# A state-space, attention and expert block on one core: the first scan block spread by TensorE, another softplus, and the causal mask on GpSimd

## The chip, the core and the metric

The kernel runs on one core of a Trainium2 chip. A core has TensorE for matrix products (PE; its weight loads, PEld, overlap them), VectorE (DVE), ScalarE (ACT), GpSimd (POOL) and SyncE (SP). Each engine works through its own list of instructions in order, and waits on semaphores for what other engines or transfers deliver. DMA transfers are issued from the queues of SP, ACT and POOL. The on-chip memory has 128 partitions; a tile written "128x512" has 512 elements in each of them. PE writes into the banks of a second memory, PSUM, from which ACT and DVE read.

The metric is the time of one execution in microseconds of the device. A profile records one execution; its span goes from the first to the last instruction.

## The reference

Input is x of 4 sequences, 1024 tokens, 128 channels. Three parts follow each other:

```python
# 1: state space (256 inner channels, 16 states), then layernorm(x + ...)
xz = x @ in_proj_w.T;  xb, z = split(xz)
xb = silu(conv_b + sum_k xpad[:, k:k+L] * conv_w[:, k])        # 4 taps
dt_in, B, C = split(xb @ x_proj_w.T)                           # 1, 16, 16
dt = softplus(dt_in * dt_w[:, 0] + dt_b)
dA = exp(dt[..., None] * -exp(A_log))
h[t] = dA[t] * h[t-1] + (xb * dt)[t] * B[t]                    # scan over tokens
y = layernorm(sum_n h * C + xb * D_param) * silu(z)
x = layernorm(x + y @ out_w.T)
# 2: attention, 16 heads of 8 channels, causal
s = (layernorm(x) -> q, k, v);  scores = q @ k.T;  scores[above the diagonal] = -max
hidden = x + softmax(scores) @ v @ o_w + o_b
# 3: 16 experts, two per token, at most 512 tokens each, 512 hidden
x = layernorm(x + hidden + experts(layernorm(hidden)))
```

## The kernel before

**Order.** No part of the order is left to the compiler. Each operation is registered with a planner (`Plan`, methods of `Emit` such as `pe`, `act`, `tt`, `scan`, `dma`), with a due time `v` as its first argument, an estimated duration and the tiles that it reads and writes. `Plan.schedule` is a list scheduler: whenever an engine comes free in its model, the ready operation with the lowest `v` is taken; for ACT an operation that needs another table of functions counts as later. The outcome is one list for each engine, issued in that order. Tiles come from pools with few slots, so an operation also waits for a slot. After the fact `Plan.run` puts filler matmuls (zeros, L1560) into gaps of PE of 800 ns or more, once the constants for them are there and while an accumulating group is open.

There are two plans. `before_branch` loads weights, makes the first of eight "fronts", and works out a bound on the attention scores (matmuls against `one_col`, a root as a power on POOL, a maximum, `mild`). Then the program branches on `mild`. `mild_path` holds the second plan: all the rest.

**A front** (`front`, 512 tokens): the convolution as four products with `w_tap` for each of two blocks of 128 channels, Silu on ACT; two products for the gate z with Silu; `xproj`, copied from PSUM as `proj` (row 0 is dt_in, rows 1 to 32 are B and C); for each channel block the `dt` product with `w_dt`, then softplus: DVE adds the bias and takes the minimum with 40 (`dtmin`, L450), ACT does Exp and Ln(1 + .), DVE takes the maximum of that and the biased input (`dt`, L457), then u = xb * dt (L437). xb, silu(z), dt, u, B and C go to DRAM (L368, by SP).

**Scans** (`scans`, nine units: seven of 512 tokens and two of 256). A partition holds one of 32 channels and one of 4 states. For each half m of the channels `dt` and `u` are read back from DRAM, each row repeated over 4 partitions (`dt_sp`, `u_sp`); B and C come likewise, repeated over the channels (`bt`, `ct`). For each group g of 4 states: one product u * B of 128x2048 on DVE, four Exp(dt * a) on ACT (`da`), four scans on DVE (L463), a copy of the state, one product h * C of 128x2048 on DVE, and products on PE with `sel` that sum over the states. The layernorms use a power of -0.5 on POOL (`rr`), which DVE's L457 and ACT then use.

**Attention.** A block of 128 keys against up to 512 queries: for groups of four heads, scores on PE into PSUM (L390), Exp on ACT into `pr` (L417), then products with v into an accumulating bank (`av`). On diagonal blocks a second product, the identity times `mask_k` (-1e38 above the diagonal, made by POOL at L1623), is added to the scores for each head:

```python
calls.append(("mm", pst[:, jj, :w], kk[:, j0 + jj, :], q[:, j0 + jj, q0:], True, not diag))
if diag:
    calls.append(("mm", pst[:, jj, :P], fx(identb), fx(mask_k), False, True))
```

Attention of a unit runs behind its scans, beside the scans of later units; what is left after the last scan runs by itself. From unit 6 (`DVE_FROM`) some copies may be taken by DVE or ACT, as the planner finds them free. `post`, `route` and `sends` follow for each unit: POOL sends token rows to the experts' buffers by indirect DMA (L2010). After all units come the experts, the fetch of their results (L2111) and the last layernorm.

Of the kernel before, what the change touches and what calls it, by code (L numbers as in the profile page):

```python
# [9 lines left out]
F32 = mybir.dt.float32  # L10
# [8 lines left out]
P = 128  # L19
# [36 lines left out]
TABLE = 1283  # L56
# [81 lines left out]
class Op:  # L138
    __slots__ = ("v", "engs", "emit", "deps", "succ", "left", "ready", "start", "end", "done", "eng", "allocs",
                 "uses", "table", "name", "wire", "seq", "opens", "closes")  # L140


class Plan:
# [17 lines left out]
    def add(self, v, engs, emit, outs, ins, name="", table=None, wire=0, free=(), after=()):  # L161
# [3 lines left out]
        op.opens = op.closes = None  # L165
        op.start = op.end = op.done = op.eng = None
# [27 lines left out]
    def schedule(self):  # L194
# [65 lines left out]
        times, queued = [0.0], {0.0}  # L260

# [7 lines left out]
        while n_left:  # L269
# [8 lines left out]
            while again:  # L278
                again = False
                for e in engines:  # L280
# [3 lines left out]
                    for op in waiting[e]:  # L284
# [6 lines left out]
                        if e == "ACT" and op.table and op.table != table:  # L291
                            v += 100.0
                        if best is not None and (v, op.seq) >= best[:2]:
                            continue
# [23 lines left out]
                    op.end = t + dur  # L318
                    op.done = op.end
# [17 lines left out]
    def run(self):  # L337
        order = self.schedule()
        last, ready, groups = 0.0, False, {}
        with self.tc.manual_schedule():  # L340
            for op in order:
                if op.eng == "PE":
                    gap = op.start - last
                    if ready and groups and gap >= FILL_GAP:
                        view = next(iter(groups.values()))
                        for _ in range(int(gap / FILL_STEP)):
                            self.fill(view)
                    last = op.end
                op.emit(op.eng)
                ready = ready or op is self.fill_after  # L350
                if op.opens is not None:
                    groups[id(op.opens.buf)] = op.opens
                if op.closes is not None:
                    groups.pop(id(op.closes.buf), None)


class Emit:
# [12 lines left out]
    def pe(self, v, calls, share=1, name="", group=None, last=False):  # L370
        nc = self.nc
        dur, outs, ins = 0.0, [], []
        for kind, out, lhsT, rhs, start, stop in calls:
# [7 lines left out]
            dur += one / 0.92 / share  # L381
            outs.append(out)
# [9 lines left out]
        op = self.p.add(v, {"PE": dur}, emit, outs, ins, name)  # L392
        if group is not None:
            op.opens, op.closes = (None, group) if last else (group, None)
# [34 lines left out]
    def _dve(self, v, emit, outs, ins, cols, per=1.0, fixed=None, name="", pool=False):  # L429
        if fixed is None:  # L430
            fixed = 125 if any(x.psum for x in outs + ins) else 62
        return self.p.add(v, {"POOL" if pool else "DVE": (fixed + per * cols / 0.96) * (2.2 if pool else 1)}, emit, outs, ins, name)

    def tt(self, v, out, a, b, op, pool=False, name=""):
        eng = self.nc.gpsimd if pool else self.nc.vector
        fixed = 600 if op == ALU.pow else None
# [41 lines left out]
    def memset(self, v, out, value, pool=False, name=""):  # L478
        eng = self.nc.gpsimd if pool else self.nc.vector
        return self._dve(v, lambda e: eng.memset(out.real(), value), [out], [], out.cols, name=name, pool=pool)  # L480
# [15 lines left out]
def mamba_then_moe_block_kernel(ctx: ExitStack, tc: tile.TileContext, a: dict, out: bass.AP):  # L496
# [847 lines left out]

    plan_a = Plan(nc, tc)
# [36 lines left out]
    conv_b, dt_b = small("f_conv_b", [P, NC2]), small("f_dt_b", [P, NC2])  # L1382
# [8 lines left out]
    def fronts_of(p, e, n_dt):  # L1391
# [9 lines left out]
        W = dict(w_in=fx(w_in), w_tap=fx(w_tap), w_xp=fx(w_xp), w_dt=fx(w_dt), conv_b=fx(conv_b), dt_b=fx(dt_b))  # L1401

        def front(f, v, step):
# [9 lines left out]
            xb = []  # L1413
            for c in range(NC2):
                pt = p.new(pool["bank"])
                e.pe(v + step, [
# [4 lines left out]
                e.act(v + 2 * step, t, pt, AF.Silu, bias=W["conv_b"][:, c : c + 1], name="xb")  # L1421
                e.dma(v + 7 * step, fx(chan["xb"][f])[c * P : (c + 1) * P, :], t, name="xb_d")
                xb.append(t)
            for c in range(NC2):
                pt = p.new(pool["bank"])
                e.pe(v + 2 * step, [("mm", pt, W["w_in"][:, DI + c * P : DI + (c + 1) * P], xT[:, NTAP - 1 :], True, True)], name="zmm")
                t = p.new(pool["sz"])
                e.act(v + 2 * step, t, pt, AF.Silu, name="sz")
                e.dma(v + 6 * step, fx(chan["sz"][f])[c * P : (c + 1) * P, :], t, name="sz_d")
            pt = p.new(pool["bank"])  # L1430
            e.pe(v + 3 * step, [("mm", pt, W["w_xp"][:, c, :], xb[c], c == 0, c == NC2 - 1) for c in range(NC2)], name="xproj")
            proj = p.new(pool["proj"])
            e.act(v + 3 * step, proj, pt, AF.Copy, name="proj")
            e.dma(v + 4 * step, fx(bc_h[f]).rearrange("s g i t -> (s g i) t"), proj[1 : 1 + 2 * NS, :], name="bc_d")
            for c in range(NC2):
# [3 lines left out]
                b1 = W["dt_b"][:, c : c + 1]  # L1439
                e.ts(v + 4 * step, ex, pt, b1, DT_MAX, ALU.add, ALU.min, name="dtmin")  # L1440
                e.act(v + 5 * step, ex, ex, AF.Exp, name="sp_exp")
                e.act(v + 5 * step, ex, ex, AF.Ln, bias=fx(one_col), name="sp_ln")
                dt = p.new(pool["dt"])
                e.stt(v + 6 * step, dt, pt, b1, ex, ALU.add, ALU.max, name="dt")
                e.dma(v + 6 * step, fx(chan["dt"][f])[c * P : (c + 1) * P, :], dt, name="dt_d")
                u = p.new(pool["u"])
                e.tt(v + 6 * step, u, xb[c], dt, ALU.mult, name="u")
                e.dma(v + 6 * step, fx(chan["u"][f])[c * P : (c + 1) * P, :], u, name="u_d")
        return front

    def before_branch():
        p, e = plan_a, ea
        fx = p.fixed
        for t, value in ((mean_col, 1.0 / DI), (one_col, 1.0), (neg_half, -0.5)):
            e.memset(0, fx(t), value, name="memset")
        def load(v, t, src, queue="SP"):
# [11 lines left out]
        load(2.2, w_dt, fx(a["dt_w"]))  # L1468
        load(2.3, dt_b, fx(a["dt_b"]).rearrange("(n p) -> p n", p=P))
        for k in range(NTAP):  # L1470
            e.tt(2, fx(w_tap)[:, k, :], fx(w_in)[:, 0:DI], fx(conv_w)[:, :, k], ALU.mult, name="w_tap")
        front = fronts_of(p, e, 2)
        front(0, 0.5, 2.5)

        pn = ps.single[0][:, 0:8].rearrange("p (t s g) -> p t s g", t=2, s=2)
        for s, w in enumerate((wq_pad, wk_pad)):
            sqw = fx(bnd[s])
            e.ts(3, sqw, fx(w), fx(ln1_w), None, ALU.mult, name="sqw")
            e.tt(3, sqw, sqw, sqw, ALU.mult, name="sqw")
            for g in range(GQ):  # L1480
                e.pe(9, [("mm", fx(pn)[:, 0, s, g : g + 1], sqw[:, g, :], fx(one_col), True, True),
# [754 lines left out]
```

## Time and profile before

| | us |
|---|---|
| median of nine runs | 1120.28 (1117.57 to 1127.39) |
| the profiled execution | 1122.07 |
| its span, first to last instruction | 1120.2 |
| mean granted clock of PE | 0.899 of full speed |
| busy: PE, DVE, ACT, POOL | 907.2, 792.9, 708.1, 226.4 |

The page's second part shows the same in 40 slices of 28 us, a digit for each tenth that an engine is busy:

```profile
PE   6378789478999999999999879999868882999920
DVE  2567989998999999999999969997404113111146
ACT  3377687256997995887997659897445561443411
POOL 2010001201001001470001430101331103455532
```

Slices 1 and 2 are the start, up to slice 28 the scans run (DVE), then the rest of attention, and from slice 35 the experts (PE). The tables of functions on ACT are loaded 35 times, 1.283 us each. In the views that follow, an arrow "out<-in" names the tiles by the program, "x4" counts instructions that were merged into a line, and a bracket gives how long the engine had been idle and what ended that.

### The profile page before, as it was taken

How to read it: one execution, taken by the hardware profiler on the slowest of the kernel's cores; microseconds unless marked ns; L12 is line 12 of the kernel's file. 1: busy time of each engine (PE TensorE's matmuls, PEld its weight loads, DVE VectorE, ACT ScalarE, POOL GpSimd, SP SyncE). 2: the span in 40 equal slices, each digit the busy share in tenths (PEclk: the TensorE clock that was granted, in tenths of full speed). 3: DMA queues.
4: the chain of work that ended last, by engine and by line, in shares of the span. 5: the costliest groups of instructions: out<-in, count | busy, mean ns of one | idle time of the engine just before them, and what ended most of it. 6: DMA issues, size and time to landing. Idle time of an engine off the chain costs nothing.

```text
span 1120.2 us, 17031 instructions
## 1 busy us (share of the span) xinstructions
PE 907.2 (81%) x6136; PEld 452.4 (40%) x6136; DVE 792.9 (71%) x1390; ACT 708.1 (63%) x1069; POOL 226.4 (20%) x337
## 2 busy tenths in 40 slices
PE   6378789478999999999999879999868882999920
PEld 2123234124434336434335423445535441777710
DVE  2567989998999999999999969997404113111146
ACT  3377687256997995887997659897445561443411
POOL 2010001201001001470001430101331103455532
PEclk9588989688999998999999989999889785999965
DMA  3775686485663654482653544339623212322153
GB/s 101 263 181 201 200 294 220 169 267 156 204 183 98 191 176 118 148 248 86 202 182 106 170 110 131 107 114 290 210 81 87 69 32 67 114 71 80 48 154 94
DMA packets 152757, 168.65 MB, mean 151 GB/s; under 512 B 23635, under 2 KB 105814, under 8 KB 152534
## 3 DMA queue, kind: packets, MB, share of 16 engines
q1 hardware_dynamic: 146262, 158.63, 47.0%
q0 software_dynamic: 4096, 8.43, 2.2%
q8 instruction: 50, 0.82, 0.3%
q10 hardware_dynamic: 2304, 0.40, 0.2%
q14 instruction: 45, 0.37, 0.1%
HBM read 110.20 MB, written 57.21 MB: 149 GB/s over the span
## 4 chain that ended last, share of the span: by engine, by line
PE 45%; DVE 25%; ACT 11%; DMA 7%; issue 6%; another core or an unknown queue 2%; POOL 1%; SPq 1%; DVEq 0%; ACTq 0%; POOLq 0%
PE bank L390 23%; PE pair L390 20%; DVE arena L463 10%; DVE arena L437 10%; ACT arena L417 9%; DVE arena L457 2%; PE bank L388 2%; SPq L368 1%; DMA arena<-in_fc_w_dram 1%; DVE smalls L487 1%; DMA xin<-rt_full 1%; DMA arena<-u_h 1%; DMA q_parts<-halves 1%; DMA eout<-rt_full 1%
## 5 line engine op out<-in xcount | busy, mean ns | idle before, releaser
L417 ACT ACTIVATE arena<-pair 128x1024 f32<-128x1024 f32 (+2 forms) x336 | 299.2, 923 | 93.3 <-PE pair L390 65.2
L437 DVE TENSOR_TENSOR arena<-arena 128x2048 f32<-128x2048 f32 (+2 forms) x155 | 305.6, 1989 | 11.8 <-DMA arena<-u_h 11.7
L417 ACT ACTIVATE arena<-arena,f_a_neg 128x512 f32<-128x512 f32 (+1 forms) x288 | 187.7, 675 | 80.0 <-DVE arena L463 63.2
L390 PE MATMUL pair<-arena 128*128 128x256 bf16 (+3 forms) x864 | 196.4, 317 | 30.2 <-ACT arena L417 23.3
L437 POOL TENSOR_TENSOR smalls<-smalls,neg_half 128x4 f32<-128x4 f32 (+2 forms) x35 | 52.7, 1505 | 633.4 <-DVE smalls L448 566.1
L390 PE MATMUL bank<-arena,vp 128*32 128x256 f32 (+3 forms) x1728 | 168.0, 470 | 9.6 <-ACT arena L417 6.9
L463 DVE TENSOR_TENSOR_SCAN arena<-arena,state 128x512 f32<-128x512 f32 (+1 forms) x160 | 160.6, 1051 | 0.0
L463 DVE TENSOR_TENSOR_SCAN arena<-arena 128x512 f32<-128x512 f32 x128 | 150.1, 1209 | 0.1
L390 PEld LDWEIGHTS <-arena 128*128 128x128 bf16 x864 | 80.4, 99 | 164.5 <-issue 141.8
L390 PE MATMUL pair<-mask_k,identb 128*128 128x128 bf16 x512 | 95.9, 221 | 0.0
L390 PE MATMUL bank<-arena,f_sel 128*32 128x512 f32 x512 | 72.2, 639 | 28.5 <-DVE arena L437 28.5
L2010 POOL DMA_INDIRECT xin<-xrow,rt_put x64 | 77.9, 1216 | 80.9 <-issue 35.3
L417 ACT ACTIVATE arena<-pair,b 128x512 f32<-128x512 f32 x64 | 40.5, 683 | 71.4 <-PE pair L390 68.7
L390 PE MATMUL pair<-xT,f_w_tap 128*128 128x512 f32 x128 | 64.6, 654 | 21.8 <-DMA xT<-in_xT_dram 17.9
L2111 POOL DMA_INDIRECT eout<-arena,to x64 | 61.3, 957 | 67.7 <-DVE arena L437 49.5
L390 PEld LDWEIGHTS bank<-arena,vp 128*32 128x32 f32 x1728 | 38.4, 110 | 70.0 <-issue 46.4
L388 PE MATMUL bank<-ident,arena 128*128 128x128 f32 x256 | 44.0, 299 | 27.9 <-DMA arena<-xin 15.9
L390 PEld LDWEIGHTS bank<-arena 128*128 128x128 f32 x512 | 59.8, 192 | 5.6 <-issue 4.3
L390 PE MATMUL bank<-arena 128*128 128x128 f32 x512 | 61.2, 277 | 0.5 <-ACT arena L417 0.4
L417 ACT ACTIVATE arena<-arena,smalls 128x128 f32<-128x128 f32 x73 | 30.3, 483 | 48.3 <-DVE smalls L457 44.0
L437 DVE TENSOR_TENSOR arena<-bank,arena 128x512 f32<-128x512 f32 (+1 forms) x25 | 16.7, 666 | 61.7 <-PE bank L390 61.7
L390 PE MATMUL pair<-arena,arena 128*128 128x512 f32 x128 | 59.2, 606 | 0.0
(184 smaller groups left out, 1090.7 us busy)
## 6 DMA issues: line engine op xcount, KB each, us to landing
arena<-k_parts SPq DMA_DIRECT2D x52, 288.0 KB
arena<-bc_h SPq DMA_DIRECT2D x56, 256.0 KB
arena<-dt_h SPq DMA_DIRECT2D x56, 256.0 KB
arena<-u_h SPq DMA_DIRECT2D x56, 256.0 KB
arena<-in_fc_w_dram SPq DMA_DIRECT2D x32, 256.0 KB
q_parts<-halves SPq DMA_DIRECT2D x21, 384.0 KB
k_parts<-halves SPq DMA_DIRECT2D x21, 384.0 KB
arena<-q_parts SPq DMA_DIRECT2D x28, 288.0 KB
```

The source lines that it names most:

```text
L368: return self.p.add(v, {queue: 460}, lambda e: engine.dma_start(out.real(), in_.real()), [out], [in_], name, wire=wire, after=after)
L388: nc.tensor.transpose(out.real(), lhsT.real(), rhs.real())
L390: nc.tensor.matmul(out.real(), lhsT=lhsT.real(), rhs=rhs.real(), start=start, stop=stop)
L417: nc.scalar.activation(out.real(), in_.real(), func, scale=real(scale), **kw)
L437: return self._dve(v, lambda e: eng.tensor_tensor(out.real(), a.real(), b.real(), op), [out], [a, b], out.cols, fixed=fixed, name=name, po ...
L457: return self._dve(v, lambda e: nc.vector.scalar_tensor_tensor(out.real(), a.real(), real(s), b.real(), op0, op1), [out], self._views(a, s ...
L463: return self._dve(v, lambda e: nc.vector.tensor_tensor_scan(out.real(), d0.real(), d1.real(), real(init), ALU.mult, ALU.add), [out], self ...
L487: self._dve(v, lambda e: nc.vector.bn_stats(s.real(), x.real()), [s], [x], 128, name=name + "_bn")
L2010: inst = nc.gpsimd.indirect_dma_start(out=dst.real()[:, :], out_offset=bass.IndirectOffsetOnAxis(ap=idx.real(), axis=0), in_=src.real(), i ...
L2111: inst = nc.gpsimd.indirect_dma_start(out=eo_d.real()[:, :], out_offset=bass.IndirectOffsetOnAxis(ap=idx.real(), axis=0), in_=src.real(), ...
```

## The change

Six things are changed together.

- *Softplus.* The bias dt_b becomes row 33 of `w_dt`, and `proj` gets a row of ones by an Identity with a column of the identity as bias. Then softplus is max(x, 0) + ln(1 + exp(-|x|)): ACT does Abs, Exp with scale -1 and Ln; `dtmin` on DVE is gone.
- *Front 0* is cut in two: `conv_half` stays ahead of the branch, `dt_half` moves behind it (`adopt` takes over its two tiles). The chain of `mild` gets earlier due times, the loads of `A_log` go from ACT's queue to SP's, and the Exp of `a_all` waits for both Silu of the convolution.
- *The first block of scans* (unit 0, m = 0) gets dt and u not from DRAM but by PE: `wide` is the identity with each column repeated four times, so a product spreads 32 rows over 128 partitions. For the first g the Exp and the products with B read that from PSUM; copies go to the tiles that later g read. Front 1 waits for it. In the built order dt and u are loaded in 68 transfers each instead of 72.
- *Mask.* The 512 mask products and their weight loads are gone. After the Exp, POOL sets `pr` above the diagonal to 0 in place (`keep_below`); from unit 6 the planner may give that to DVE. In the built order POOL does 164 (152 of them before the last scan: 102 of 256 columns, 50 of 512) and DVE 20, 19 of them after the last scan.
- *The planner* models PE's clock (`Clock`), chooses fillers while it schedules (544 filler products instead of 456, 56 of them ahead of the first work of front 0), lets ACT hold its table for 3 us before it changes, and has other estimates for powers and memsets on POOL. Table loads go from 35 to 19.
- Some small operations on POOL (`tokcol`, `pad`) get other due times.

```diff
-TABLE = 1283
+TABLE, HOLD = 1283, 3000
...
                         if e == "ACT" and op.table and op.table != table:
                             v += 100.0
+                            if t < op.ready[e] + HOLD:
+                                wake(op.ready[e] + HOLD)
+                                continue
...
+                    if e == "PE":
+                        gap = t - last
+                        if ready and (groups or spare) and gap >= FILL_GAP:
+                            op.fillers = int(gap / FILL_STEP)
+                            clock.fill(last, gap, op.fillers)
...
+    def keep_below(self, v, x, lower, dve=False, name=""):
+        nc, n = self.nc, x.shape[1]
+        engs = {"POOL": 130 + 1.05 * x.cols}
+        if dve:
+            engs["DVE"] = 62 + x.cols / 0.96
+
+        def emit(e):
+            if e == "POOL":
+                nc.gpsimd.affine_select(out=x.real(), in_=x.real(), compare_op=ALU.is_ge, fill=0.0, base=0,
+                                        pattern=[[0, n], [1, P]], channel_multiplier=-1)
+            else:
+                nc.vector.tensor_tensor(x.real(), x.real(), lower.real().unsqueeze(1).to_broadcast([P, n, P]), ALU.mult)
+
+        return self.p.add(v, engs, emit, [x], [x] + ([lower] if dve else []), name)
...
-            e.act(v + 3 * step, proj, pt, AF.Copy, name="proj")
+            e.act(v + 3 * step, proj, pt, AF.Identity, bias=fx(ident)[:, 1 + 2 * NS : 2 + 2 * NS], name="proj")
...
-                b1 = W["dt_b"][:, c : c + 1]
-                e.ts(v + 4 * step, ex, pt, b1, DT_MAX, ALU.add, ALU.min, name="dtmin")
-                e.act(v + 5 * step, ex, ex, AF.Exp, name="sp_exp")
+                e.act(v + 4 * step, ex, pt, AF.Abs, name="sp_abs")
+                e.act(v + 5 * step, ex, ex, AF.Exp, scale=-1.0, name="sp_exp")
                 e.act(v + 5 * step, ex, ex, AF.Ln, bias=fx(one_col), name="sp_ln")
                 dt = p.new(pool["dt"])
-                e.stt(v + 6 * step, dt, pt, b1, ex, ALU.add, ALU.max, name="dt")
+                e.stt(v + 6 * step, dt, pt, 0.0, ex, ALU.max, ALU.add, name="dt")
...
+        load(2.2, w_dt[n_row : n_row + 1], fx(a["dt_b"]).unsqueeze(0))
...
-        front = fronts_of(p, e, 2)
-        front(0, 0.5, 2.5)
+        conv_half, _, _ = fronts_of(p, e, 2)
+        conv_half(0, 0.5, 2.5)
...
-            e.dma(20, a_all[:, j, :], fx(a["A_log"])[j * NR : (j + 1) * NR, :].unsqueeze(1).to_broadcast([NR, NI, NS]),
-                  queue="ACT", name="a_all")
+            e.dma(4, a_all[:, j, :], fx(a["A_log"])[j * NR : (j + 1) * NR, :].unsqueeze(1).to_broadcast([NR, NI, NS]),
+                  name="a_all")
...
-        e.act(21, a_all, a_all, AF.Exp, name="a_all")
+        e.act(21, a_all, a_all, AF.Exp, name="a_all").deps.add(conv_half.last[1][1])
...
+        xb_first = [adopt("xb") for _ in range(NC2)]
+        first = dt_half(0, 0.0, 2.0, xb_first, kept=(0,))
...
+                    spread = own and g == 0
+                    if spread:
+                        wide = new("tmp", "wide")
+                        e.copy(1, wide.rearrange("p (m i) -> p m i", i=NI), fx(ident).unsqueeze(2).to_broadcast([P, P, NI]), name="wide")
+                    for j in range(J if spread else 0):
+                        lhsT = wide[:, j * P : (j + 1) * P]
+                        for src, dst, k in ((first[0][0], dts[j], 0), (first[0][1], us[:, j, :], 1)):
+                            pb = new("bc")
+                            mm = e.pe(12 + 0.1 * j + 0.05 * k, [("mm", pb, lhsT, src, True, True)], name="spread")
+                            if k:
+                                e.tt(12 + 0.1 * j, h[:, j, :], pb, bt[g], ALU.mult, name="uB")
+                            else:
+                                d_first.append(new("da"))
+                                ex = e.act(12 + 0.1 * j, d_first[j], pb, AF.Exp, scale=fx(a_neg)[:, j, 0:1], name="da")
+                            e.act(14 + j, dst, pb, AF.Copy, dve=True, name="spread_c")
+                    for conv, gate in second_front if spread else ():
+                        conv.deps.add(mm)
+                        gate.deps.add(ex)
...
-                            calls.append(("mm", pst[:, jj, :w], kk[:, j0 + jj, :], q[:, j0 + jj, q0:], True, not diag))
-                            if diag:
-                                calls.append(("mm", pst[:, jj, :P], fx(identb), fx(mask_k), False, True))
+                            calls.append(("mm", pst[:, jj, :w], kk[:, j0 + jj, :], q[:, j0 + jj, q0:], True, True))
...
+                        if diag:
+                            half = pr[:, 0:per, :P]
+                            e.keep_below(vv + 0.1 * j0 + dv * 0.4, half, fx(lower), dve=u >= DVE_FROM, name="mask")
```

## The prediction

> **What bounds the kernel now.** I first cut the span into stages by the first and last instruction of each kind: scans run from 47.25 to 773.8 us, the last front ends near 192, the experts start near 949. The busy time of each engine in each stage (window; length, then PE, weight load, DVE, ACT, POOL with instruction counts; clock, DMA share, GB/s):
>
> ```profile
> 44.85:195.00 150.15, 125.95 (x408) 51.61 (x412) 127.66 (x126) 107.15 (x143) 11.13 (x9) 0.90 0.71 226
> 195.00:742.50 547.50, 483.78 (x3610) 216.59 (x3598) 525.70 (x709) 422.96 (x657) 90.82 (x90) 0.94 0.53 161
> 742.50:948.80 206.30, 157.50 (x1385) 87.70 (x1383) 79.39 (x324) 109.39 (x163) 42.51 (x77) 0.84 0.39 113
> 948.80:1071.00 122.20, 121.37 (x696) 88.25 (x696) 17.99 (x37) 47.20 (x73) 62.56 (x120) 0.99 0.27 79
> ```
>
> DVE is busy 525.7 of 547.5 us in the second row, so DVE sets the pace there although PE has more busy time over the whole kernel. In the first row DVE idles 22.5 us, in the third PE works through attention left over, in the fourth PE is full. The page's chain of waits says the same (PE 45%, DVE 25%, ACT 11%). Second view, what DVE waits for between 45 and 756 us (total, times, longest):
>
> ```profile
> DVE arena L450 <- PE pair L390: 15.7, 4, 6.3
> DVE arena L437 <- DMA arena<-u_h: 11.7, 1, 11.7
> DVE arena L457 <- ACT arena L417: 7.5, 10, 2.1
> DVE arena L450 <- ACT arena L417: 2.7, 1, 2.7
> ```
>
> L450 is the `dtmin` of a front: DVE works its list in order, so scans behind it stand while it waits for the front's matmul. The `u_h` wait is the start, and the timeline shows it:
>
> ```profile
> 31.41 1.28 DVE L437 TENSOR_TENSOR arena<-arena 128x512 f32<-128x512 f32 x2
> 34.70 2.48 SPq L368 DMA_DIRECT2D arena<-dt_h  x4
> 37.28 2.49 SPq L368 DMA_DIRECT2D arena<-u_h  x4
> 44.85 2.29 DVE L437 TENSOR_TENSOR arena<-arena 128x2048 f32<-128x2048 f32 x1 [11.73 <-DMA arena<-u_h]
> 47.25 4.57 DVE L463 TENSOR_TENSOR_SCAN arena<-arena 128x512 f32<-128x512 f32 x4
> ```
>
> The first `u` is made by 32.7 us, but its way through DRAM lets the first long DVE instruction start at 44.85 only.
>
> **The terms**, against the profiled execution's span of 1120.2 us.
>
> *1. Start: -15.* In the new order, from rows of before: first conv at 10.87 (the 16 instructions of both channel blocks took 7.12, so 3.56 a block), its Silu 0.69, second conv 3.56 behind that Silu's bank, Silu 0.69: 19.4. Table load 1.28 and the `a_all` Exp 0.31: 21.0. Branch, 0.8 us from `mild` written (24.26) to the branch's first instruction (25.04): 21.8. `proj` 0.58, `dt` matmul 1.9 (3.78 for both blocks): 24.3. Abs 0.60, Exp 0.63, second Abs 0.60, Ln 0.66: 26.8. L457 0.74 and `u` 0.66: 28.2. Spread matmul 0.9 (two instructions of 7.12/16), multiply from PSUM 0.68: the first scan stands at 30 instead of 47.25. Then each of the four channel groups needs an Exp from PSUM (0.68) and copies (6 of 8 on ACT, 0.6 to 0.7), about 2.5 us a group against 1.12 a scan, so the fourth scan ends near 38.8 instead of 51.82, with the second step's multiply (2.27) already used as filling: -13 to -18, taken -15. It falls to -10 if the first B rows, which still come by DRAM, are late (loads of this kind took 3.0 to 7.5 us from issue to use, and seven loads stand before them on SP), or if the 56 new filler matmuls ahead of the first conv leave the clock lower: 16 passes took 9.47 us cold at 45.91, 7.12 at 10.87.
>
> *2. Front stalls: -14.* The 14 `dtmin` in the branch go, and with them 15.7 + 2.7 = 18.4 us of waits. ACT's Abs reads the matmul instead. What is late next is L457, which needs the Ln; it waited 7.5 us in ten pieces. ACT in the first row gains 14 x 0.60 = 8.4 for Abs and loses 16 table loads of 1.283 = 20.5 (38.4 before), so it is no nearer its bound. I keep a quarter of the waits, at L457; the ends are -4 (they mostly move there) and -20.
>
> *3. DVE's own work: -8.6.* 14 x 0.743 (the row of L450 `dtmin`) = -10.4; the first product as 4 x 0.68 instead of 2.29: +0.4; two spread copies on DVE, 2 x 0.69: +1.4. DVE is the pace-setter, so this counts in full while it stays so.
>
> *4. Mask on PE: -4.* 512 mask matmuls go, each with a weight load. What one takes on PE is the spacing, not its 221 ns of mean duration:
>
> ```profile
> 768.91 0.22 PE L390 MATMUL pair<-arena 128*128 128x128 bf16 x1
> 768.97 0.22 PE L390 MATMUL pair<-mask_k,identb 128*128 128x128 bf16 x1
> 769.03 0.22 PE L390 MATMUL pair<-arena 128*128 128x128 bf16 x1
> ```
>
> 0.06 from start to start. The 384 in the scan stage (21 us of PE) free nothing: DVE covers them. Without that cover they would be worth the 21. The 128 behind it are on the path of the third row: 128 x 0.055 = -7. Against that stand new masks between Exp and the value matmul, 12 on POOL and 19 on DVE; where 12 groups end on such a block I let 0.25 us each show, after the 0.28 row below: +3. Ends -7 and +6, if half of 31 masks show 0.4 us in full.
>
> *5. POOL beside DVE: +20.* The open cost. 152 masks lie on POOL in the scan stage: 102 of 256 columns, 50 of 512. No row of before has such an instruction there. The nearest of its kind and the nearest of its situation:
>
> ```profile
> 26.30 0.28 POOL L1623 TENSOR_SCALAR_AFFINE_SELECT mask_k<-mask_k 128x128 bf16<-128x128 bf16 x1
> 59.53 1.25 DVE L463 TENSOR_TENSOR_SCAN arena<-arena 128x512 f32<-128x512 f32 x1
> 59.64 1.21 POOL L476 COPY arena<-arena 1x64 f32<-1x64 f32 x1
> 60.70 1.24 DVE L463 TENSOR_TENSOR_SCAN arena<-arena 128x512 f32<-128x512 f32 x1
> 60.80 1.21 POOL L476 COPY arena<-arena 1x64 f32<-1x64 f32 x1
> 61.86 1.24 DVE L463 TENSOR_TENSOR_SCAN arena<-arena 128x512 f32<-128x512 f32 x1
> ```
>
> Scans alone start 1.12 us apart (four in 4.55 at 105.97); beside these 64-column copies 1.165: each copy costs DVE 0.045, and itself stretches until the scan ends. Lower bound, that much per mask whatever its width: 152 x 0.045 = 7. By width, 0.18 for 256 and 0.36 for 512 columns: 102 x 0.18 + 50 x 0.36 = 36. Upper bound, the whole moving part at the rate of the 128-column row over POOL's cheapest row of 0.14: (0.28 - 0.14)/128 = 1.1 ns a column, so 102 x 0.28 + 50 x 0.56 = 57. A mask can only take time between two DVE instructions that would have followed without a gap: in the new order 195 of DVE's 357 long instructions in this stage are followed directly by another long one. I take 36 x 195/357 = 20, nearest to the row by width.
>
> The Trainium skill speaks against this change in "SBUF — State Buffer", section "Who interferes with whom": a DVE instruction with two SBUF inputs and a GpSimd instruction that reads SBUF exclude each other, for the whole instruction. The trace agrees that POOL stretches (a 128x8 power took 2.47 us beside scans), but the scans beside that power kept their pace, 2.33 us for two, so no whole power of over 1 us was held against DVE. By the rule in full (0.14 more for each of 152 masks than the upper bound) the term would be 57 + 21 = 78 and the sum +39; by the row it is the 20 above.
>
> *6. POOL's queue: +3.* The masks stand in POOL's list between 35 powers of the normalisations and 64 sends. DVE's L457 waits for a power; that wait was 1.1 us before. If every power stood behind one mask of 0.5 us it would be 35 x 0.5 = 18; the powers have due times ahead of DVE's use, so 3, ends 0 and 18. The sends feed the experts after 949 and have slack until then.
>
> *At nothing:* the eight `A_log` loads moved to SP (ahead of the front's stores, seven took 4.55 us of ACT's queue; SP waits for the front's data at that time anyway, and without that cover they are 5 us at the start, inside term 1's bound); 88 more filler matmuls (in PE gaps; PE is not the bound before 742); table loads in the scan stage, covered by DVE.
>
> Sum: -15 - 14 - 8.6 - 4 + 20 + 3 = -18.6, span 1101.6. The execution took 1.87 us beyond its span and lies 1.8 above the median, so as a median 1101.7, given as 1102. The gains are 41.6 us: the masks eat them when one costs 41.6/152 = 0.27 us of DVE.
>
> **Rivals.**
> A, slower: POOL holds DVE for the whole moving part of every mask (57 instead of 20): -18.6 - 20 + 57 = +18.4, 1139. For it: copies stretch to the scan's end, so the two do exclude each other. Against: the scans beside powers. It decides from 0.27 us a mask.
> B: the cost is per mask and not per column (7): 1120.2 - 31.6, as a median 1089. For it: the power rows, which hold DVE for next to nothing whatever their length.
> C: the stalls only move. ACT's chain Abs, Exp, Ln, shared with the scans' own Exps, leaves L457 waiting (-4), and the start is bound by the B rows (-10): -10 - 4 - 8.6 - 4 + 23 = -3.6, 1117, at the edge of no change. For it: L457 already waited ten times for ACT.
>
> **How the numbers follow.** Forecast 0.40 (its own range 1094 to 1110), A 0.20, B 0.28, C 0.12. About 0.3%, 3.4 us, is what a measurement tells from no change (the nine runs spread 0.9%). Faster: 0.40 + 0.28 + 0.04 of C = 0.72; same: 0.06 of C and 0.02 of A = 0.08; slower 0.20. All low ends together give 1075, all high ones far above A; the range 1078 to 1137 holds B and most of A and leaves out about 2 in 10.
>
> **What would show it.** First scan at about 30 us and the fourth's end near 39; no wait of DVE for the matmul in the front stage, and less than 10 us at L457; DVE's busy time in scans and 128x2048 products up by some 20 us in total or gaps that end with masks (A: nearly 60; B: under 10); masks on POOL of 0.4 and 0.7 us alone and over 1 us beside DVE; waits for powers below 5 us; the stretch from the last scan to the experts about 4 us shorter than 175. The forecast is wrong if scans spread to over 1.4 us beside masks, or if the first scan comes after 36.

## The result, and the profile after

| | before | changed |
|---|---|---|
| median, us | 1119.58 (31 runs) | 1144.48 (10 runs) |
| ratio, 95% interval | | 1.0212 (1.0181 to 1.0243) |
| span of the profiled execution | 1120.2 | 1139.1 |
| first scan starts, last scan ends | 47.25, 773.8 | 35.41, 807.9 |
| last scan to first product of the experts | 172.9 | 158.6 |

Slower by 25 us by the medians. In the two traces the start is 11.8 us earlier and the end of the scans 34 us later; 14 us of that come back behind them. The stages again, cut in the same way (length, then PE, weight load, DVE, ACT, POOL with counts; clock, DMA share, GB/s):

```profile
44.85:195.00 150.15, 124.55 (x466) 50.54 (x465) 131.02 (x135) 103.87 (x158) 13.78 (x9) 0.93 0.71 229
195.00:760.00 565.00, 470.13 (x3090) 187.29 (x3089) 515.06 (x668) 401.99 (x616) 255.17 (x221) 0.94 0.48 146
760.00:967.00 207.00, 157.67 (x1346) 81.61 (x1344) 106.95 (x357) 117.44 (x182) 67.20 (x103) 0.88 0.41 121
967.00:1090.00 123.00, 121.11 (x691) 87.50 (x690) 17.31 (x36) 48.72 (x75) 61.77 (x118) 0.99 0.27 78
```

In the second row DVE now idles 49.9 us (565.0 - 515.06) where it idled 21.8, and POOL is busy 255 us where it was 91. (Of the 21.8, 9.0 are a single wait of L457 at 656 us that the profile puts to "remote". The prediction's view of waits leaves it out, and the trace of the same kernel on another chip, b_before, has no such wait.) The groups of the changed kernel by shape, DVE's long ones and then POOL's masks:

```profile
L474 DVE TENSOR_TENSOR arena<-arena 128x2048 f32<-128x2048 f32 x127 | 292.4, 2316 | 8.8 <-issue 7.5 <-PE bank L426 1.2
L500 DVE TENSOR_TENSOR_SCAN arena<-arena 128x512 f32<-128x512 f32 x128 | 156.1, 1251 | 0.3
L500 DVE TENSOR_TENSOR_SCAN arena<-arena,state 128x512 f32<-128x512 f32 x96 | 120.5, 1297 | 0.0
L500 DVE TENSOR_TENSOR_SCAN arena<-arena,state 128x256 f32<-128x256 f32 x64 | 46.4, 768 | 1.2 <-ACT arena L454 1.2
...
L527 POOL TENSOR_SCALAR_AFFINE_SELECT arena<-arena 128x256 f32<-128x256 f32 x104 | 104.9, 1024 | 248.0 <-ACT arena L454 246.8 <-DMA arena<-bc_h 0.7 <-DMA arena<-dt_h 0.2
L527 POOL TENSOR_SCALAR_AFFINE_SELECT arena<-arena 128x512 f32<-128x512 f32 x60 | 80.5, 1355 | 106.4 <-ACT arena L454 104.9 <-DVE smalls L505 1.4
```

Before, the four DVE groups had means of 2275, 1209, 1265 and 729 ns: each long instruction is 32 to 42 ns longer in the mean, and the longest scan takes 1.65 us where it took 1.28. A mask of 256 columns takes 0.40 us at the least and 1.02 in the mean, one of 512 columns 0.63 and 1.36. What DVE waits for between 45 and 774 us:

```profile
DVE smalls L509 <- PE bank L424: 19.8, 9, 5.6
DVE arena L494 <- ACT arena L454: 12.9, 10, 2.8
DVE arena L494 <- PE bank L426: 7.6, 5, 2.5
DVE arena L474 <- issue: 7.5, 1, 7.5
DVE rt_full L485 <- DMA xin<-rt_full: 3.8, 3, 2.6
DVE smalls L494 <- POOL smalls L474: 3.7, 3, 2.0
```

The waits of `dtmin` are gone. New at the top is L509, the reciprocal of a softmax's sum (0.6 us before): it needs attention's products with v, and those wait for masks. The timeline shows one such place, a short one:

```profile
281.30 0.41 POOL L527 TENSOR_SCALAR_AFFINE_SELECT arena<-arena 128x256 f32<-128x256 f32 x1 [0.23 <-ACT arena L454]
...
282.54 7.06 POOL L527 TENSOR_SCALAR_AFFINE_SELECT arena<-arena 128x256 f32<-128x256 f32 x4 [0.84 <-ACT arena L454]
...
284.04 2.29 DVE L474 TENSOR_TENSOR arena<-arena 128x2048 f32<-128x2048 f32 x1
...
286.65 0.84 PE L426 MATMUL bank<-arena,vp 128*32 128x384 f32 x4 [1.57 <-POOL arena L527]
...
288.12 1.94 ACT L454 ACTIVATE arena<-pair 128x1024 f32<-128x1024 f32 x2 [2.93 <-POOL arena L527]
...
291.63 0.26 DVE L509 RECIPROCAL smalls<-bank 128x16 f32<-128x16 f32 x1 [0.95 <-PE bank L424]
```

Four masks take 7.06 us beside DVE's products and scans. PE waits for one; ACT waits 2.93 us, because its next exponentials need a buffer that POOL still holds; 9 us after the first of these masks DVE stands at the reciprocal, with scans queued behind it.

The longest waits arise where POOL issues its sends (`DMA_INDIRECT`, 1 to 3 us each, two batches of 16 before the last scan). POOL works in order too, so a mask behind sends waits for them, and with it the product with v:

```profile
474.33 1.88 POOL L2110 DMA_INDIRECT xin<-xrow,rt_put  x1 [0.21 <-DVE arena L500]
...
476.51 1.93 POOL L2110 DMA_INDIRECT xin<-xrow,rt_put  x1 [0.22 <-issue]
...
478.46 1.69 POOL L527 TENSOR_SCALAR_AFFINE_SELECT arena<-arena 128x256 f32<-128x256 f32 x1
...
480.21 3.53 PE L426 MATMUL bank<-arena,vp 128*32 128x512 f32 x8 [10.04 <-POOL spacer L2109]
...
487.72 2.29 DVE L474 TENSOR_TENSOR arena<-arena 128x2048 f32<-128x2048 f32 x1 [7.55 <-issue]
```

ACT has stood idle since 470.8, so the exponentials were ready by then. PE stands for 10.04 us at a product with v, and the products with `sel` of the scans stand behind it in PE's list; DVE then waits 7.55 us with its next long product. This is the 7.5 put to "issue" above; b_after's trace has the same wait, 7.7 us, put to PE.

### The profile page after: what moved, and what is told of

The parts are those of the page before. It is cut to its first block, busy times and chain, and to the rows that moved or that the text cites. A ratio compares the mean times of both kernels' runs of the same rounds, so it can differ in the third digit from the quotient of the medians.

```text
span 1139.1 us, 16476 instructions
## 1 busy us (share of the span) xinstructions
PE 910.4 (80%) x5728; PEld 422.4 (37%) x5728; DVE 821.3 (72%) x1403; ACT 697.0 (61%) x1072; POOL 419.9 (37%) x501
## 4 chain that ended last, share of the span: by engine, by line
PE 42%; DVE 19%; POOL 13%; ACT 11%; issue 7%; DMA 6%; another core or an unknown queue 1%; SPq 0%; ACTq 0%; POOLq 0%; DVEq 0%
PE bank L426 21%; PE pair L426 19%; ACT arena L454 10%; DVE arena L500 7%; POOL arena L527 7%; DVE arena L474 6%; POOL xin L2110 4%; DVE arena L494 2%; PE bank L424 2%; POOL smalls L474 1%; DMA arena<-in_fc_w_dram 1%; DMA arena<-u_h 1%; DVE smalls L539 1%; DMA q_parts<-halves 1%
## 5 line engine op out<-in xcount | busy, mean ns | idle before, releaser
L454 ACT ACTIVATE arena<-pair 128x1024 f32<-128x1024 f32 (+2 forms) x352 | 306.6, 908 | 133.9 <-PE pair L426 92.6
L527 POOL TENSOR_SCALAR_AFFINE_SELECT arena<-arena 128x256 f32<-128x256 f32 (+1 forms) x164 | 184.9, 1145 | 354.4 <-ACT arena L454 351.7
L426 PE MATMUL bank<-arena,vp 128*32 128x256 f32 (+3 forms) x1728 | 193.9, 483 | 54.9 <-POOL arena L527 36.8
L454 ACT ACTIVATE arena<-arena,f_a_neg 128x512 f32<-128x512 f32 (+1 forms) x284 | 184.1, 672 | 62.1 <-DVE arena L500 48.6
L426 PE MATMUL pair<-arena 128*128 128x256 bf16 (+3 forms) x864 | 174.3, 321 | 33.2 <-ACT arena L454 25.3
L500 DVE TENSOR_TENSOR_SCAN arena<-arena,state 128x512 f32<-128x512 f32 (+1 forms) x160 | 166.9, 1085 | 1.2 <-ACT arena L454 1.2
L500 DVE TENSOR_TENSOR_SCAN arena<-arena 128x512 f32<-128x512 f32 x128 | 156.1, 1251 | 0.3
L426 PEld LDWEIGHTS <-arena 128*128 128x128 bf16 x864 | 70.3, 100 | 170.5 <-issue 146.2
L474 POOL TENSOR_TENSOR smalls<-smalls,neg_half 128x4 f32<-128x4 f32 (+2 forms) x35 | 60.5, 1730 | 162.8 <-DVE smalls L485 141.8
L2110 POOL DMA_INDIRECT xin<-xrow,rt_put x64 | 81.2, 1269 | 38.5 <-DVE rt_put L474 15.2
L426 PE MATMUL pair<-xT,f_w_tap 128*128 128x512 f32 x128 | 59.7, 611 | 0.6 <-ACT arena L454 0.6
```

The costliest lines, as they stand in the source:

```text
L426: nc.tensor.matmul(out.real(), lhsT=lhsT.real(), rhs=rhs.real(), start=start, stop=stop)
L454: nc.scalar.activation(out.real(), in_.real(), func, scale=real(scale), **kw)
L474: return self._dve(v, lambda e: eng.tensor_tensor(out.real(), a.real(), b.real(), op), [out], [a, b], out.cols, fixed=fixed, name=name, po ...
L500: return self._dve(v, lambda e: nc.vector.tensor_tensor_scan(out.real(), d0.real(), d1.real(), real(init), ALU.mult, ALU.add), [out], self ...
L527: nc.gpsimd.affine_select(out=x.real(), in_=x.real(), compare_op=ALU.is_ge, fill=0.0, base=0, pattern=[[0, n], [1, P]], channel_multiplier=-1)
L2110: inst = nc.gpsimd.indirect_dma_start(out=dst.real()[:, :], out_offset=bass.IndirectOffsetOnAxis(ap=idx.real(), axis=0), in_=src.real(), i ...
```

## The experiments

Each was run in turns with the kernel before on its chip. That took 1120 to 1123 us on some chips and 1090 to 1092 on others (for the most part between the last scan and the experts: 172.9 us at a granted clock of 0.82 in the first trace, 150.3 at 0.88 in b_before's; why, stays open). So only numbers from chips of one kind are subtracted. Chips A are those with 1120 us below, chips B those with 1091. The ranges of e5 to e8 were written with times of A and ran on B; they are read as differences.

| label | edit | median, us | ratio (95%) |
|---|---|---|---|
| on chips A | | | |
| e1_pe_mask | changed, mask on PE | 1096.6 | 0.9776 (0.9737 to 0.9815) |
| e2_pool_mask | before, mask on POOL | 1169.8 | 1.0433 (1.0398 to 1.0467) |
| e3_skip | changed, POOL's masks not issued | 1084.1 | 0.9655 (0.9618 to 0.9692) |
| e4_memset | changed, memset in their place | 1103.5 | 0.9826 (0.9789 to 0.9862) |
| on chips B | | | |
| b_before | before | 1091.7 | 1.0001 (0.9981 to 1.0021) |
| b_after | changed | 1126.0 | 1.0338 (1.0277 to 1.0399) |
| b_pe_mask | as e1 | 1068.1 | 0.9778 (0.9733 to 0.9824) |
| b_skip, c_skip | as e3 | 1068.0, 1065.8 | 0.9775 (0.9734 to 0.9815), 0.9777 (0.9746 to 0.9808) |
| e5_scratch | masks read, nobody waits for the result | 1111.9 | 1.0163 (1.0122 to 1.0204) |
| e12_lock_only | POOL reads a constant, nothing waits | 1105.1 | 1.0136 (1.0108 to 1.0165) |
| e6_cost | changed, planner told the masks' durations | 1116.5 | 1.0214 (1.0177 to 1.0252) |
| e9_hybrid | mask on PE for units 0 to 5 | 1066.3 | 0.9760 (0.9725 to 0.9794) |
| e7_softplus | before, new softplus alone | 1093.2 | 1.0015 (0.9992 to 1.0039) |
| e11_old_softplus | as e1, old softplus | 1077.2 | 0.9884 (0.9845 to 0.9923) |
| e10_no_hold | as e1, ACT holds no table | 1074.4 | 0.9833 (0.9786 to 0.9880) |
| e8_no_spread, b_no_spread | as e1, first block by DRAM | 1082.9, 1081.2 | 0.9899 (0.9865 to 0.9934), 0.9910 (0.9879 to 0.9941) |

**Is it the mask?** Put back in the changed kernel, put alone into the kernel before, left out:

```diff
 e1_pe_mask
...
+ if diag:
+     calls.append(("mm", pst[:, jj, :P], fx(identb), fx(mask_k), False, True))
...
- e.keep_below(..., half, fx(lower), dve=u >= DVE_FROM, name="mask")
 e3_skip, in keep_below
+ if e == "POOL" and name == "mask":
+     pass
```

> The changed kernel with the mask set on PE again, all else as changed. Theory M (the masks on POOL cost the time, twice: DVE's long instructions stretch beside them, 17 us in the trace, and the products with v wait for them, so that DVE's reciprocals, in order in its list, wait 20 us where they waited 1): the rest of the change keeps its gain, start 8 to 12 us, stalls 7, DVE work 9, so 1090 to 1100. Rival P (the planner's new order, with the held table of ACT and the clock model, makes the waits): little changes, 1130 to 1145.

> The kernel before with only the mask moved behind the exponential on POOL (from unit 6 on POOL or DVE), old planner, old start, old softplus. Theory M: slower by as much as the mask cost in the changed kernel, 30 to 45 us, so 1150 to 1165. Rival P: 1115 to 1125.

> The changed kernel with the same lists in the same order, but POOL's mask instructions are not issued (attention is then not causal on the diagonal blocks of the first six units and wherever POOL had them later). Theory M: all of the mask's cost goes, 1090 to 1105. Rival P: the order stays, so the waits stay, 1130 to 1145.

Theory M held three times: 1096.6; 1169.8, a little above its range; 1084.1, below it. The rest of the change is a gain of 2.2%, and the mask on POOL costs about 60 us (1144.5 against 1084.1). The lists of the changed kernel without POOL's masks have hardly any such waits (2.2 us at L509, where the masks made it 19.8), so the order as such is not the cause.

**How does it cost?** The changed kernel, e3 and e4 run the same 883 DVE instructions between first and last scan. The windows over that stretch, changed, e3, e4:

```profile
35.41:807.86 772.45, 649.98 (x3895) 261.61 (x3895) 701.15 (x883) 555.19 (x860) 290.12 (x250) 0.94 0.53 162
```

```profile
34.47:748.78 714.31, 620.35 (x3851) 261.02 (x3893) 676.37 (x883) 553.69 (x860) 119.85 (x98) 0.95 0.56 175
```

```profile
36.24:766.79 730.55, 625.70 (x3852) 260.07 (x3893) 676.37 (x883) 554.57 (x860) 165.11 (x250) 0.95 0.55 171
```

DVE's busy time differs by 701.15 - 676.37 = 24.8 us, that is 0.163 us for each of 152 masks; its idle time (length less busy) by 71.3 - 37.9 = 33.4. So the cost is two-fifths stretching and three-fifths waiting. Of the stretching, some 17 us are the long instructions above; the rest is in short ones. In the kernel before the split is alike: from first to last scan e2's DVE is busy 711.6 us, where it was 682.2, and idle 75.4, where it was 44.3.

Most of the waiting lies where the sends are. Two windows, each from the start of a batch of sends to some 10 us behind its end, in the changed kernel and then in e3:

```profile
452.00:498.00 46.00, 31.89 (x196) 10.76 (x193) 32.81 (x43) 28.01 (x40) 35.94 (x41) 0.85 0.46 142
647.00:692.00 45.00, 36.40 (x216) 13.60 (x216) 34.87 (x49) 30.13 (x45) 35.67 (x41) 0.92 0.44 129
```

```profile
436.00:479.00 43.00, 38.77 (x276) 14.66 (x274) 42.06 (x61) 39.00 (x56) 30.46 (x33) 1.00 0.66 210
608.00:649.00 41.00, 38.37 (x253) 14.71 (x256) 39.68 (x63) 35.65 (x53) 31.24 (x34) 0.96 0.58 171
```

DVE idles 13.2 and 10.1 us there with masks, 0.9 and 1.3 without: 21 of the 33.4 us. No run moves the sends away from the masks, so this share is read from the traces and not tested.

> The changed kernel with the same lists, but where POOL masked it sets the same 256 or 512 columns to 1 by a memset, which writes SBUF and reads nothing (the diagonal blocks then weigh all keys alike). The dependence of the products with v stays. If DVE and POOL exclude each other only when POOL reads: scans keep their 1.21 us, a memset takes about 0.5 us, and the time comes near that without masks, 1095 to 1110. If writes exclude each other too: 1130 to 1145.

A memset in the masks' place, with the same dependences, leaves DVE's busy time as it is without masks, to the second decimal. POOL's groups of that run:

```profile
L527 POOL MEMSET arena<- 128x256 f32 x104 | 32.3, 314 | 298.0 <-ACT arena L454 296.9 <-PE bank L426 1.0
L527 POOL MEMSET arena<- 128x512 f32 x60 | 31.1, 528 | 125.3 <-ACT arena L454 123.7 <-DVE smalls L505 1.5
```

POOL's writes neither stretch DVE nor are they stretched: 0.31 and 0.53 us where the mask took 1.02 and 1.36. Of the 60 us, 41 go with the reading (a select that DVE leaves alone is only 0.1 us longer than a memset). The other 19 (16 us of DVE's idle time) are what even a short step on POOL costs in these lists: over its two batches of sends (437 to 480 and 621 to 661 us) e4's DVE idles 17.0 us, 14.7 more than e3's, so nearly all of it arises at the sends.

```diff
 e5_scratch: reads the exponentials, writes bytes elsewhere
+ nc.gpsimd.affine_select(out=scr[:, 0:120*n], in_=x[:, :, 0:120], ...)
 e12_lock_only: reads a constant instead
+ nc.gpsimd.affine_select(out=scr[:, 0:120*n], in_=lower[:, 0:120] repeated n times, ...)
```

> The changed kernel with the same lists, but POOL's mask instruction reads the exponentials (120 of each 128 columns) and writes them as bytes to a tile that nobody reads: it still runs beside DVE and still waits for the exponential, but the products with v no longer wait for it (attention is then not causal where POOL masked). Theory M splits the mask's 60 us (1144 against 1084 without) into DVE's stretching, 17 us by the durations, and waits for late masks: 1100 to 1110, scans still near 1.25 us. If sharing SBUF with DVE is most of it: 1125 to 1145. If writing four bytes for each element makes the stretching: scans at 1.21 us and 1085 to 1092.

> The changed kernel's lists, where POOL's mask instruction reads the constant triangle (120 of 128 columns, repeated for each head) and writes bytes to a tile that nobody reads: POOL reads as often beside DVE, but nothing waits for a mask, and no buffer of exponentials is held (attention is then not causal where POOL masked). If the mask's cost is DVE's stretching plus lateness as the traces say, 25 and 33 us: about 25 us above the run without masks on the same chip, with scans near 1.25 us. If lateness is only another face of the stretching: 45 to 60 above. If POOL, running ahead in bursts, meets DVE less: 10 to 20 above.

> The lists without POOL's masks, on the same chip as the run above. 0.966 to 0.978 of before, as on the two chips so far.

On chips B, from first to last scan, DVE's busy and idle time: without masks 676.5 and 34.6 (c_skip); reading a constant 699.7 and 45.9; reading the exponentials 698.6 and 57.1; the change itself 701.0 and 68.0 (b_after). Stretching is 22 to 25 us in all three. Lateness comes in three steps of about 11 us, one trace each (two traces without masks differ by 2.5). What comes late differs: in e12 powers (below), in e5 exponentials whose buffers POOL holds, and with the full mask the products with v. e5 was expected 16 to 26 us above the run without masks and came 45 above (1111.9 against 1067, the mean of b_skip and c_skip), since I had left out the buffers that POOL holds (ACT waits 17.1 us for POOL's selects in its trace); e12's 39 us above c_skip fit none of its three cases: the stretching came as expected, the queue had been forgotten. DVE's waits in e12, first line, and the same line of c_skip:

```profile
DVE smalls L494 <- POOL smalls L474: 17.9, 3, 9.3
```

```profile
DVE smalls L494 <- POOL smalls L474: 2.4, 2, 1.5
```

There POOL takes masks that wait for nothing, and powers stand behind them and behind the sends: the two longest waits, 7.05 us at 500 and 9.3 at 684, come just after a batch of sends, the second behind a copy that itself waited 6.4 us for a send to land. In the changed kernel that wait is 3.7 us, and the reciprocals wait instead.

```diff
 e6_cost
- engs = {"POOL": 130 + 1.05 * x.cols}
+ engs = {"POOL": 610 + 1.78 * x.cols}
```

> The changed kernel with one number changed: the planner takes a mask on POOL as 1.07 us for 256 and 1.52 us for 512 columns, as the trace had them, instead of 0.40 and 0.67, and lays out its lists by that. If the waits come from lists that were laid out for masks that are too fast, a good part of the 43 us beside DVE's stretching goes: 1110 to 1130. If they come from the masks as such, 1138 to 1150.

It was expected 14 to 34 us below the changed kernel; on chips B it is 10 below (1126.0). Lists that reckon with slow masks wait less (DVE idles 57.5 us from first to last scan, where it idled 68.0 in b_after), but most of the cost stays.

> The kernel before itself, with its trace, beside three others on one chip, because the kernel before took 1092 us on the chip of the last four runs and 1120 to 1123 on the two chips before. Ratio 1.00. If the difference between chips lies in one stage, the trace shows it: in the runs on that chip the stretch from the last scan to the experts was 148 us where the first trace had 173.

> The changed kernel on the same chip as the next two. If ratios carry over between chips: 1.021 again, whatever this chip's time of before; if not, differences between kernels have to be read within one chip only.

> The changed kernel with the mask on PE: 0.978 of before if ratios carry over.

> The changed kernel with its lists, POOL's masks not issued, once more, beside three others. On one chip (kernel before 1092 us) the changed kernel took 1126.0 and the one with PE's mask 1068.1. If lists and not chips decide, this one takes 1052 to 1058 there, so that POOL's masks cost some 70 us and PE's 12; in ratios 0.966 of before.

The ratio of the kernel with PE's mask carries over (0.9776, 0.9778), that of the changed kernel does not (1.0212, 1.0338): on chips B the change is worse, by 34 us. The kernel without POOL's masks is 12.5 us faster than the one with PE's mask on a chip A (e1 to e3), and no faster on B (1068.1 to 1068.0), so b_skip missed its range, and POOL's masks cost 58 there, not 70.

> The changed kernel with the mask on PE for the units whose attention runs beside scans (0 to 5), and behind the exponential on POOL or DVE for the last three. Theory M: beside the scans POOL's masks cost 60 us and PE's nothing that shows; behind the last scan PE is the bound and DVE is free, so there the moved mask is worth the 7 us of step 4, as intended: 0.971 to 0.976 of before, against 0.978 with all masks on PE. If masks behind the exponential are late there too: 0.978 to 0.985.

No difference from all masks on PE that these runs can tell. Both beat the kernel before and the changed one; the hybrid's ratio is the lowest of the causal variants by 0.002, inside its interval.

**What the rest is worth.**

```diff
 e8_no_spread (on e1)
...
- own = u == 0 and m == 0
+ own = False
 e10_no_hold (on e1)
- TABLE, HOLD = 1283, 3000
+ TABLE, HOLD = 1283, 0
 e7_softplus (on before; e11 undoes the same on e1)
- e.ts(v + 4 * step, ex, pt, b1, DT_MAX, ALU.add, ALU.min, name="dtmin")
+ e.act(v + 4 * step, ex, pt, AF.Abs, name="sp_abs")
...
```

> The changed kernel with the mask on PE, and the first block of scans by DRAM again instead of spread by PE. If the earlier start is worth what the trace shows at the fourth scan, 8 to 10 us against the 1096.6 with spread: 1103 to 1108. If later slack swallows it: 1095 to 1099. If the first blocks' stay in DRAM costs the full 15 of my step 1: 1110 to 1115.

> The same with the first block through DRAM again. Against the run above on the same chip: 8 to 12 us slower if the earlier start is worth what the first scans show; equal within 4 us if later slack swallows it.

On one chip 1081.2 against 1068.1: with the spread the kernel is 13 us faster than without, a little more than expected (e8, on another chip B, gives the same ratio). But the kernel without it starts later than the kernel before: on that chip the fourth scan ends at 60.0 us, in the kernel before at 55.7, with the spread at 47.2.

> The kernel before with the new softplus alone (bias as a row of the weights, Abs on ACT, no minimum on DVE). My step 2 and 3: DVE loses 10.4 us of work and 14 of 18.4 us of waits: 1095 to 1100. What the trace of the changed kernel says, where 15 us of waits stand at the next DVE instruction of the same chain (3.6 before): 10.4 plus 7, so 1100 to 1108. If ACT's additional work makes the scans' own exponentials late: 1115 to 1125.

> The kernel with PE's mask (0.978), but the old softplus with the minimum on DVE. By my steps 2 and 3 it loses 10 us of DVE work and some of the stalls: 0.990 to 1.000. If the new softplus is worth nothing in any plan: 0.975 to 0.982.

> The kernel with PE's mask (0.978), but ACT does not hold its table in the plan (HOLD 0). If the new softplus only pays because of the held table (alone it was 1.0015 of before, with 27 us of waits for ACT in front of the instruction that makes dt): 0.990 to 1.000. If the hold matters little: 0.975 to 0.982.

Alone, the new softplus gives nothing, and its trace says why; DVE's waits between 44 and 800 us:

```profile
DVE arena L457 <- ACT arena L417: 27.4, 11, 6.5
DVE arena L437 <- DMA arena<-u_h: 10.7, 1, 10.7
DVE arena L463 <- ACT arena L417: 6.8, 2, 6.5
```

The wait went from `dtmin` to `dt`, which stands behind Abs, Exp, Ln and table loads on ACT. In the changed plan, undoing it costs 9 to 12 us (1077.2 against 1068.1, 0.9884 against 0.9778) and undoing the held table about 6 (0.9833; the intervals overlap, so this is likely and not shown). Both came between their two cases.

## Why the prediction was wrong

The step that failed is 6, "POOL's queue: +3", with ends 0 and 18. It had the right queue and the wrong waiter: it counted powers behind masks, and what came late was masks behind sends and attention behind masks, with DVE's reciprocals and long products at the end of that: 33.4 us of idle time against a bound of 18. It counted the sends and gave them slack; it did not ask what stands behind them. Step 4 had allowed 0.25 us at 12 group ends for the latency of a mask, and only behind the last scan; the scan stage has no such term, although DVE's list holds attention's reciprocals between scans. Of the 42.8 us between 1101.7 and 1144.5, steps 4 to 6 make some 29 (48 where they summed to 19) and steps 1 to 3 some 13 (25 where they summed to 37.6).

1. *Start, -15*: too large. By its own measure, the fourth scan's end with 2.3 for the product already done, it is 8 on A (46.3 against 51.8) and 11 on B (47.2 against 55.7); the 13 of the spread alone count from a later start. The first scan came at 35.41, not 30. The last Ln before the first `dt` ended at 26.84, against 26.8, by luck: the first convolution began 1.0 us earlier than in my working and took 5.38 instead of 3.56, and the `dt` products took 1.98 instead of 3.78 for both blocks. Then DVE stood in front of `w_out_b` until 28.34, for a constant's load, PE in front of a bias product until 30.57, and the spread itself, 0.9 in my working, was slow: the second bank was there at 34.06, and the first multiply stood behind ACT's copy of it:

```profile
26.13 0.71 ACT L454 ACTIVATE arena<-arena,one_col 128x512 f32<-128x512 f32 x1
```

```profile
28.34 0.48 DVE L485 TENSOR_SCALAR w_out_b<-w_out,ln_b 128x128 f32<-128x128 f32 x2 [4.47 <-DMA ln_b<-in_ln_b_dram]
28.74 0.68 DVE L494 SCALAR_TENSOR_TENSOR arena<-pair,arena 128x512 f32<-128x512 f32 x1
...
34.68 0.69 DVE L474 TENSOR_TENSOR arena<-bank,arena 128x512 f32<-128x512 f32 x1 [0.91 <-ACT arena L449]
35.41 1.23 DVE L500 TENSOR_TENSOR_SCAN arena<-arena 128x512 f32<-128x512 f32 x1
```

```profile
9.86 5.38 PE L426 MATMUL pair<-xT,f_w_tap 128*128 128x512 f32 x8
...
30.57 0.38 PE L426 MATMUL bank<-one_col,arena 1*128 1x1 f32 x2 [4.07 <-POOL arena L513]
30.88 5.67 PE L426 MATMUL bank<-arena,arena 128*128 128x512 f32 x8
```

2. *Stalls, -14*: too large. 22.0 us of waits of a front's two DVE steps (18.4 and 3.6) became 15.2 at `dt`: -7. Rival C's -4 was nearer.
3. *DVE's work, -8.6*: right; from first to last scan b_pe_mask has 675.3 us of it and b_before 682.6, so -7.3.
4. *Mask on PE, -4*: right in sign. From the last scan to the experts the changed kernel takes 158.6 us and e1 167.8 (-9.2, on A), b_after 143.9 and b_pe_mask 148.5 (-4.6, on B), one trace each. Its high end of +6 leaves out the -7 beside it; together they make -1.
5. *POOL beside DVE, +20*: right in size, 24.8. The price by width, scaled with the share of exposed instructions, stood closer than either bound; that the price goes by width no run shows. (The upper bound took 0.14 us for POOL's cheapest row; the trace has 0.09, which would make it 77.) Its sign of being wrong, scans of over 1.4 us, did come, in 20 of 288 scans. The Trainium skill's rule ("SBUF — State Buffer", "Who interferes with whom") showed on the other side, in POOL's masks of 1.0 to 1.4 us in the mean; on DVE's side the rule in full, priced at 78 us in the prediction, was three times too much (0.163 us a mask, where one alone takes 0.40 to 0.63). That a GpSimd instruction which only writes does not contend, as the same section has it, e4 bears out (676.37 us of DVE's work with and without memsets). What I had not drawn from it is that a POOL that is held up holds up those who wait for POOL.
6. *Table loads in the scan stage, "at nothing"*: the held table is likely worth 6 us, since ACT stands in front of `dt`.

Steps 1 to 3 summed to -37.6; the kernel that has them and PE's mask, e1, gained 25 us (2.24% of 1120), and the parts as measured, 8 to 11, 7 and 7.3, make 22 to 25. Steps 4 to 6 summed to +19; the move of the mask cost 48 on A (1144.5 against 1096.6) and 58 on B. Rival A had the sign and nearly the time (1139), but by 57 us of stretching, where 25 were found: near by the wrong mechanism.

## What to carry to other kernels

Before work moves to an engine that already has work, price its duration there beside the pacing engine (here 2.5 times the duration alone for 256 columns), look at what stands ahead of it in that engine's list (here sends), and then follow who waits for the result until the chain comes back to the pacing engine's own list. Two runs with the same lists, one without the suspect instruction, split the cost at once: the difference in busy time is contention, the difference in idle time is lateness. A stall that an edit removes is only gone if the next instruction of the same chain is ready earlier.

## What the runs showed of the hardware that was not expected

GpSimd's reading lengthened VectorE's long instructions by 32 to 42 ns in the mean, and short ones too: a 128x4 state copy from 160 ns without masks (c_skip) to 190 (e12), a 128x4 scalar_tensor_tensor from 145 to 273. A select of 240 columns took 1.34 us in the mean and one of 480 took 1.30 (e12), where the shortest took 0.38 and 0.60, so beside VectorE the width did not set the time there. And one and the same program differed by 2.5% between chips, 22.6 of 28.6 us between the last scan and the experts.
